# Attention beside a ternary feed-forward layer: gate and up kept as signs, the weights and half of the layer norm behind the first heads

## The chip, the cores and the metric

The kernel runs on one core of one Trainium2 chip. The metric is the device time of one execution in microseconds (us), and the median of several runs is compared. A core has a matrix engine (TensorE, PE), a vector engine (VectorE, DVE), a scalar engine for activations (ScalarE, ACT), a general engine (GpSimd, POOL), an engine that mostly issues DMAs (SyncE, SP), and 16 DMA engines. Each engine works off its own instructions in order, and instructions of different engines wait for each other by semaphores.

## The reference

The input x holds 2 sequences of 1024 tokens with 512 features, in f32. All of it, shortened:

```python
xn = layernorm(x)                       # over the 512 features, no affine part
q, k, v = split(xn @ w_qkv.T + b_qkv)   # 32 heads of 16 features
scores = q @ k.T / 4 + slope[head] * (key - 1023)   # ALiBi
scores = where(causal, scores, -1e9)
s = softmax(scores) @ v                 # per head
s = s @ w_out.T + b_out
# octonion layer: w has 8 components; M[k, i] is +w[j] or -w[j], with j given by k and i
ternary(w) = scale * clip(round(w / scale), -1, 1)   # scale = mean |w|
gate, up = xn @ M(ternary(w_gate)), xn @ M(ternary(w_up))   # 512 -> 8 x 170 = 1360
g = silu((silu(gate) * up) @ M(ternary(w_down)))            # 1360 -> 512
out = x + s * g
```

Ternary weights are kept as -1, 0 and 1, and the scale is multiplied in when a product is read out. The 512 by 1360 matrices of gate and up consist of 8 by 8 blocks, each a signed copy of one of the 8 components.

## The kernel before

The hidden width of 1360 makes 11 tiles `mt` of 128 (the last has 80 rows). The 2048 tokens make 16 tiles of 128 for the layer norm and 4 blocks `tb` of 512 for the feed-forward part. Everything is emitted in one long function. PE keeps the order in which its instructions are emitted. The order on the other engines, and the semaphores, are set by the scheduler of the framework, from priorities and data dependencies.

**Head.** `load_x` (L174) fetches the tokens and `normal` (L203) normalises them: statistics on DVE, Sqrt on ACT (L211), scaling on DVE (L214). `norm_item` (L354) transposes four blocks of 128 on PE (tile ptx) and copies them out with ACT (L360) into xnT. `load_wq` and `compact_wq` (L117 to L134) bring the q and k weights of two pairs of heads (wqr) and pack them on POOL into wq. `add_ring` (L139) makes the operand tiles, four q_stack and five k_stack, and fills their fixed rows with memsets (L142 to L147). q and k are kept as two parts, high and low, which add up to the f32 value.

**Attention.** Work goes in 32 units: sequence, group of four heads, half of the queries. `qk_items` (L417) computes q and k of two groups (pqk L436) and splits them (st: ACT L448, DVE L449). They go to DRAM and come back arranged as stacks by DMAs of the SP queue (`fill_q`, `fill_k`, L470 to L490). `max_items` (L492) makes the scores once (s L504) for their row maxima (DVE mp L514, scr L517). `place_max` (L543) transposes the maxima (pm) and ACT copies them to mr (L556), which four small POOL DMAs place into q_stack (L558). `exp_step` (L568) makes the scores again (s L578, mask L589) and ACT exponentiates them into p (L593). `value_step` (L595) multiplies with v (po L606), where v comes from `v_items` (L378, pv L391), and `normalise` (L619) divides. `out_items` (L645) is the output projection of one block.

**Ternary weights.** For each of w_g, w_u and w_d: `load_weight` (L259) loads 64 rows and once more with neighbouring components swapped; `ternary_sum` and `ternary_total` (L271, L277) compute the scale from wsum (DVE L274) through a product on PE (tot, L280); `ternary_signs` (L287, DVE L292 and L293) leaves -1, 0 or 1. `expand` (L295) makes 8 signed copies for each of four row blocks on ACT (L302), through two buffers "m". For gate and up, `expand_in` (L307) writes the full matrices from there into the DRAM array mw by POOL DMAs (L311, L315). For down, `turn_down` (L319) transposes first, four tiles at a time (ptd L329, ACT md, POOL L333).

**The planner.** At the time of writing the program, a loop with a rough model of engine times chooses what PE does next. Attention steps are taken in order. `side` is a list of other PE work with positions counted in steps from which it may be taken and by which it is due. `behind` is a queue of work that `later` appends, taken one at a time when what it needs is known (`next_behind`).

**Tail.** For each block of 512 tokens `split` (L1181) makes the high and low part of xnT (POOL L1189, DVE L1190). For the first block `load_fw` (L1193) fetches for each `mt` a tile fw with twelve slots of 128 columns: four gate, four up, four down. Eight of the eleven use the freed stack tiles. All four blocks use the same fw. `gate_up` (L1198) makes the products pg and pu (L1206), silu on ACT (L1215), the product on DVE (L1217) and the split hs on ACT and POOL (L1222, L1223). `down` (L1226, pd L1240) follows two `mt` behind. `load_rest` (L1260) fetches what the result needs.

Of the kernel before, what the change touches and what calls it, by code (L numbers as in the profile page):

```python
# [59 lines left out]
def kernel(  # L60
# [52 lines left out]
    mw = dram.tile([NM, P, 12, P], F32, name="mw")  # L113
# [25 lines left out]
    def add_ring(pool, qs, ks):  # L139
        for n in range(qs):  # L140
            q = pool.tile([P, 4, 512], F32R, name=f"q_stack{len(q_ring)}")
            nc.gpsimd.memset(q[64:128].bitcast(F32), 0.0)  # L142
            nc.gpsimd.memset(q[64:66].bitcast(F32), 1.0)
            q_ring.append(q)
        for n in range(ks):
            k = pool.tile([P, 4, 512], F32R, name=f"k_stack{len(k_ring)}")
            nc.gpsimd.memset(k[64:128].bitcast(F32), -1.0)  # L147
            k_ring.append(k)
# [20 lines left out]
    tmp = head.enter_context(tc.tile_pool(name="tmp", bufs=2))  # L169
# [4 lines left out]
    def load_x(t, eng):  # L174
        if t < 8:

            tag = ("ot", "ot", "oT", "oT", "y", "y", "posb", "scr")[t]
            xt = wk.tile([P, D], F32, tag=tag, name=f"xt_{t}", bufs=2 - t // 6)
        else:
            xt = tmp.tile([P, D], F32, tag="xt", name=f"xt_{t}", bufs=4)  # L180
        eng.dma_start(out=xt, in_=x[t * P : (t + 1) * P, :])
        x_tiles[t] = xt

    for t in range(8):
        load_x(t, nc.sync)
    load_wv(0)
    load_wq((0, 0), nc.scalar)
    al_sb = tmp.tile([P, HID], F32, tag="q", name="al", bufs=1)[0:H, 0:S]
    nc.gpsimd.dma_start(out=al_sb, in_=calibi)
    for n in range(2):  # L190
        for i in range(4):
            nc.gpsimd.dma_start(
# [4 lines left out]
            )  # L197
    nc.gpsimd.dma_start(out=mask, in_=cmask)
    nc.gpsimd.dma_start(out=bv_sb, in_=bv.partition_broadcast(P))

# [58 lines left out]
    def load_weight(src, name):  # L259
        if name == "g":  # L260
            w = vp.tile([P, 8, H8], F32, tag="v", name="w_g")
        else:
            w = tmp.tile([P, 8, H8], F32, tag="w", name=f"w_{name}")
        nc.sync.dma_start(out=w[0:64].rearrange("p j o -> p (j o)"), in_=src)
        pairs = src.rearrange("p (j s o) -> p j s o", s=2, o=H8)
        swapped = w[64:128].rearrange("p (j s) o -> p j s o", s=2)
        for n in range(2):
            nc.sync.dma_start(out=swapped[:, :, n, :], in_=pairs[:, :, 1 - n, :])
# [18 lines left out]
    def ternary_signs(name):  # L287
# [3 lines left out]
        q = tmp.tile([P, HID], F32, tag="q", name=f"q_{name}", bufs=1)  # L291
# [3 lines left out]
    def expand(name, kt, dtype):  # L295

        w = w_tiles[name]
        signs = sgn["d" if name == "d" else "i"]
        m = tmp.tile([P, 8, H8], dtype, tag="m", name=f"m_{name}_{kt}")

        for k in range(8):
            nc.scalar.activation(  # L302
                m[:, k, :], w[:, k ^ kt * 2, :], AF.Identity, scale=signs[:, kt, k : k + 1]
            )
        return m

    def expand_in(name, kt):  # L307
        m = expand(name, kt, F32R).rearrange("p k o -> p (k o)").bitcast(F32)
        slot = kt + (4 if name == "u" else 0)
        full = HID // P  # L310
        nc.gpsimd.dma_start(  # L311
            out=mw[0:full, :, slot, :].rearrange("m p n -> p m n"),
            in_=m[:, 0 : full * P].rearrange("p (m n) -> p m n", n=P),
        )
        nc.gpsimd.dma_start(out=mw[full, :, slot, 0 : HID - full * P], in_=m[:, full * P : HID])  # L315

    downs_box = {}

    def expand_down(kp):  # L319
        downs_box["nat"] = expand("d", kp, F32)  # L320

    def turn_down(kp, first):

        nat = downs_box["nat"].rearrange("p k o -> p (k o)")
        last = min(first + 4, NM)
        pt = ps_m.tile([P, 4, P], F32, tag="m", name=f"ptd_{kp}_{first}")
        for mt in range(first, last):
            fs = min(P, HID - mt * P)
            pe(nc.tensor.transpose(pt[:fs, mt - first, :], nat[:, mt * P : mt * P + fs], ident))  # L329
        md = tmp.tile([P, 4, P], F32R, tag="md", name=f"md_{kp}_{first}")  # L330
# [3 lines left out]
            out=mw[first : first + full, :, 8 + kp, :].rearrange("m p n -> p m n"),  # L334
            in_=md[:, 0:full, :].bitcast(F32),
        )
        if last == NM:
            fs = HID - (NM - 1) * P
            nc.scalar.copy(md[:fs, full, :], pt[:fs, full, :])
            nc.gpsimd.dma_start(out=mw[NM - 1, 0:fs, 8 + kp, :], in_=md[:fs, full, :].bitcast(F32))  # L340

    def alibi_parts():

        for n in range(2):
            part = tmp.tile([P, 8, H8], F32R, tag="m", name=f"al_{n}")
            part = part.rearrange("p k o -> p (k o)")[0:H, 0:S]
# [5 lines left out]
            nc.gpsimd.dma_start(out=al_dram[n], in_=part.bitcast(F32))  # L352
# [394 lines left out]
    for b in range(B):  # L747
        for hh in range(2):
            n = 2 * b + hh
            u = 8 * n  # L750
            if n == 0:
# [3 lines left out]
                max(u - 7, -1),  # L755
                u - 1,
                lambda n=n: n < 2 or unit_of(vals, V[0]) >= 8 * (n - 1),
            )
        for gp in range(2 - 2 * b, NP):
# [6 lines left out]
                lambda n=n: n < 2 or fills[0] >= 4 * (2 * n - 2),  # L766
            )
        for n, qc in enumerate((0, 1) if b + 1 < B else (1, 0)):
# [10 lines left out]
            )  # L779

# [19 lines left out]
    lead_in, behind = [], []  # L800
    grown, known = [0.0], {}
# [7 lines left out]
    def later(emit, model=None, need=None, cost=0, kind="none"):  # L809
        behind.append((emit, model, need, cost, kind))  # L810

    def grow(t):
        grown[0] = max(grown[0], t, now[0]) + 3500
        return grown[0]
# [4 lines left out]
    def weight(name, last):  # L819
# [11 lines left out]
        for kt in range(4):  # L831
            later(
                lambda kt=kt: expand_down(kt) if last else expand_in(name, kt),
                lambda kt=kt: set_known(("e", name, kt), grow(known["w", name])),
            )
            for f in range(0, NM if last else 0, 4):
                later(lambda kt=kt, f=f: turn_down(kt, f), None, ("e", name, kt), 436, "t")
# [9 lines left out]
    def end_head():  # L847
        head.close()
        add_ring(ctx.enter_context(tc.tile_pool(name="late", bufs=1)), 2, 3)

    qk, vs = qk_items(0, 0), v_items(0, 0)
    alibi_parts()
    for t in range(4):
        normal(t)
    compact_wq((0, 0))
    add_ring(early, 1, 1)
    for t in range(4, 8):
        normal(t)
    known.update({("n", t): 5500 + 1600 * t for t in range(8)})
    for name, w in (("g", wg), ("u", wu)):  # L860
        load_weight(w, name)
    add_ring(early, 1, 1)
    make_mask()
    make_signs()
    known.update({("l", "g"): 25000, ("l", "u"): 30000, ("l", "d"): 35000})
    for t in range(8, 12):
        later(lambda t=t: load_x(t, nc.sync))
    later(lambda: load_weight(wd, "d"))
    later(lambda: nc.sync.dma_start(out=bo_sb, in_=bo.partition_broadcast(P)))
    later(lambda: nc.sync.dma_start(out=wo_sb, in_=wo.rearrange("(k p) n -> p k n", p=P)))  # L870
# [8 lines left out]
    weight("g", False)  # L879
    weight("u", False)  # L880
    more_tokens(range(8, 12))
    later(lambda: [load_x(t, nc.sync) for t in range(12, 16)])
    weight("d", True)
    more_tokens(range(12, 16))
    later(end_head)
    side = [(d, ok or (lambda: True), it) for d, ok, it in lead_in + side]
# [47 lines left out]
    def try_fill():  # L934
# [4 lines left out]
        if n == 1 and len(q_ring) < 4 or part == 2 and len(k_ring) < 2:  # L939
# [153 lines left out]
    def next_behind():  # L1093
        while behind and not behind[0][3] and known.get(behind[0][2], 0) <= now[0]:
            emit, model = behind.pop(0)[:2]
            emit()
            if model:
                model()
        if not behind or not behind[0][3]:
            return []  # L1100
        emit, model, need, cost, what = behind[0]

        def go():
            behind.pop(0)
            emit()
            run_pe("F", ready, cost)
# [260 lines left out]
```

## Time and profile before

| | before |
|---|---|
| median of 3 runs | 1224.62 us |
| lowest, highest | 1218.01, 1227.27 us |
| profiled execution, its own time | 1222.66 us |
| its span | 1220.9 us |
| PE busy | 1094.6 us (90%) |
| DVE, ACT, POOL busy | 600.5, 508.3, 233.1 us |
| DMA | 113.36 MB, 93 GB/s on average |

The profile describes one execution. Busy time counts the instructions of an engine, and the idle time before an instruction is put down to what it waited for. L12 is line 12 of the kernel before. A DMA is listed by where its data go and come from (mw<-m_g). The page divides the span into 40 equal slices with a digit of tenths for each engine, and another for the granted PE clock.

### The profile page before, as it was taken

The page shows a single profiled execution, that of the slowest core. Times are in us where ns is not written, and L with a number is a line of the kernel's source. Part 1 is how long each engine was busy: PE and PEld are TensorE (multiplying, and loading weights), DVE is VectorE, ACT ScalarE, POOL GpSimd, SP SyncE. Part 2 cuts the span into 40 slices and gives each one's busy share as a digit, 9 for nine tenths or more (in the row PEclk, how much of TensorE's full clock was granted, in tenths as well). Part 3 has the DMA queues.
Part 4 walks back from the last instruction along what each step waited for, and adds up shares of the span by engine and source line. Part 5 has one row for each costly group of instructions (what it writes and reads, how often), then busy time and mean ns, then how long its engine had stood idle before and what let it go on. Part 6 is the DMA issues. An engine that isn't in the chain of part 4 may idle for free.

```text
span 1220.9 us, 16626 instructions
## 1 busy us (share of the span) xinstructions
PE 1094.6 (90%) x5714; PEld 686.8 (56%) x5714; DVE 600.5 (49%) x1640; ACT 508.3 (42%) x1131; POOL 233.1 (19%) x398
## 2 busy tenths in 40 slices
PE   4728879999799999998999999999989999999997
PEld 2414535555455555554655555555455777777775
DVE  6516506765565656666656654666732113131221
ACT  1263653345255544453543544446553222222222
POOL 6431450200111011020101000000110113232222
PEclk9868989999799999999999999999989999999998
DMA  9864456441731635416416332742217111112020
GB/s 260 220 174 138 143 91 113 110 79 40 144 59 24 114 58 127 98 52 133 74 55 128 60 74 57 173 81 41 62 49 242 42 53 51 53 35 69 20 85 35
DMA packets 78372, 113.36 MB, mean 93 GB/s; under 512 B 29472, under 2 KB 33056, under 8 KB 78288
## 3 DMA queue, kind: packets, MB, share of 16 engines
q1 hardware_dynamic: 68704, 94.10, 34.5%
q0 software_dynamic: 9296, 17.16, 4.9%
q8 instruction: 45, 0.74, 0.3%
q10 hardware_dynamic: 288, 1.05, 0.3%
q14 instruction: 39, 0.32, 0.1%
HBM read 73.76 MB, written 37.98 MB: 92 GB/s over the span
## 4 chain that ended last, share of the span: by engine, by line
PE 69%; DMA 10%; DVE 7%; issue 5%; POOL 4%; ACT 4%; SPq 0%; DVEq 0%; ACTq 0%; POOLq 0%
PE s L578 12%; PE s L504 12%; PE po L606 11%; PE pqk L436 6%; PE pg L1206 6%; PE pu L1206 5%; PE pd L1240 5%; DMA q_stack<-mr 5%; PE pout L675 4%; DVE scr L517 3%; PE pv L391 2%; PE s L589 2%; PE pm L549 1%; DVE mp L514 1%; DMA mw<-m_g 1%
## 5 line engine op out<-in xcount | busy, mean ns | idle before, releaser
L593 ACT ACTIVATE p<-s 128x512 f32<-128x512 f32 (+3 forms) x768 | 323.4, 495 | 313.9 <-PE s L589 217.1
L504 PE MATMUL s<-k_stack,q_stack 126*128 126x512 f32 (+3 forms) x768 | 306.6, 439 | 13.5 <-DVE mx L517 5.6
L578 PE MATMUL s<-q_stack,k_stack 128*128 128x512 f32 (+3 forms) x768 | 248.6, 388 | 25.4 <-DMA q_stack<-mr 19.0
L504 PEld LDWEIGHTS s<-k_stack,q_stack 126*128 126x128 f32 x768 | 141.2, 192 | 127.8 <-DVE mx L517 54.3
L514 DVE TENSOR_REDUCE mp<-s 128x1 f32<-128x512 f32 x256 | 169.0, 686 | 83.3 <-PE s L504 81.7
L578 PEld LDWEIGHTS s<-q_stack,k_stack 128*128 128x128 f32 x768 | 141.9, 193 | 96.9 <-ACT p L593 33.1
L517 DVE CUSTOM_DVE_ANT_0 scr<-s,mask 128x128 f32<-128x128 f32 (+3 forms) x256 | 125.1, 489 | 125.2 <-PE s L504 107.5
L517 DVE CUSTOM_DVE_ANT_0 scr<-s,mask,mp 128x128 f32<-128x128 f32 (+3 forms) x256 | 140.7, 550 | 85.2 <-PE s L504 67.2
L558 POOL DMA_DIRECT2D q_stack<-mr x128 | 63.6, 503 | 522.1 <-ACT mr L556 411.1
L606 PE MATMUL po<-p,v 128*32 128x512 f32 (+3 forms) x1536 | 148.2, 498 | 0.0
L436 PE MATMUL pqk<-xnT,wq 128*128 128x512 f32 x256 | 135.2, 632 | 12.7 <-ACT mr L556 6.0
L1217 DVE SCALAR_TENSOR_TENSOR h<-pu,sc_u,sg 128x512 f32<-128x512 f32 (+1 forms) x44 | 33.0, 751 | 168.8 <-PE pu L1206 163.0
L391 PE MATMUL pv<-wv,xnT 128*128 128x256 f32 x256 | 74.6, 399 | 25.0 <-ACT xnT L360 23.8
L1223 POOL TENSOR_TENSOR hs<-h,hs 128x512 fp32r<-128x512 f32 (+1 forms) x44 | 56.9, 1292 | 198.8 <-ACT hs L1222 198.8
L606 PEld LDWEIGHTS po<-p,v 128*32 128x32 f32 x1536 | 42.8, 110 | 65.8 <-issue 55.5
L1215 ACT ACTIVATE sg<-pg,sc_g 128x512 f32<-128x512 f32 (+1 forms) x44 | 30.3, 688 | 103.0 <-PE pg L1206 98.1
L436 PEld LDWEIGHTS pqk<-xnT,wq 128*128 128x128 f32 x256 | 46.1, 200 | 39.5 <-issue 22.3
L589 PE MATMUL s<-mask,ident 128*128 128x128 bf16 x512 | 66.7, 225 | 0.0
L391 PEld LDWEIGHTS pv<-wv,xnT 128*128 128x128 f32 x256 | 45.1, 194 | 34.5 <-ACT xnT L360 24.2
L675 PE MATMUL pout<-wo_sb,oT 128*128 128x512 f32 x128 | 61.9, 600 | 0.9 <-ACT oT L666 0.5
L1222 ACT CAST hs<-h 128x512 fp32r<-128x512 f32 (+1 forms) x44 | 27.2, 619 | 75.4 <-DVE h L1217 75.4
L449 DVE SCALAR_TENSOR_TENSOR st<-pqk,bqk_sb,st 128x512 fp32r<-128x512 f32 x32 | 23.8, 747 | 45.1 <-ACT st L448 44.9
(147 smaller groups left out, 1116.2 us busy)
## 6 DMA issues: line engine op xcount, KB each, us to landing
sp<-st SPq DMA_DIRECT2D x32, 512.0 KB, 3.9
q_stack<-sp SPq DMA_DIRECT2D x128, 128.0 KB, 6.1
k_stack<-sp SPq DMA_DIRECT2D x128, 128.0 KB, 4.9
wqr<-in_wqk_dram POOLq DMA_DIRECT2D x14, 512.0 KB, 6.0
xt<-in_x_dram SPq DMA_DIRECT2D x16, 256.0 KB, 8.4
att<-o SPq DMA_DIRECT2D x32, 128.0 KB, 4.8
ot<-att SPq DMA_DIRECT2D x16, 256.0 KB, 2.6
proj<-y SPq DMA_DIRECT2D x16, 256.0 KB, 3.3
```

The source lines that it names most:

```text
L391: nc.tensor.matmul(ps[:, 0:256], lhsT=xnT[:, c, b * S + kt * P : b * S + (kt + 1) * P], rhs=wv_tiles[2 * b + hh][:, c, :], start=(c == 0), ...
L436: nc.tensor.matmul(ps, lhsT=wq_tiles[b, gp][:, kt, which, :], rhs=xnT[:, kt, b * S + c * 512 : b * S + (c + 1) * 512], start=(kt == 0), st ...
L504: nc.tensor.matmul(ps[:, :n], lhsT=q_of(b, g, qc)[0 : NR - 2, i, tl * P : (tl + 1) * P], rhs=k_of(b, g, c)[0 : NR - 2, i, :n], start=True, ...
L514: nc.vector.tensor_reduce(pm, ps, AX.X, ALU.max)
L517: nc.vector.tensor_tensor_reduce(out=scr[:, :n], in0=ps[:, :n], in1=mask[:, 512 - n : 512], scale=1.0, scalar=pm if qc else -3.0e38, op0=A ...
L558: nc.gpsimd.dma_start(out=q[NR - 2 : NR, i, :].bitcast(F32), in_=mr[2 * i : 2 * i + 2, :].bitcast(F32),)
L578: nc.tensor.matmul(ps[:, :w], lhsT=k[0:NR, i, kt % 4 * P : (kt % 4 + 1) * P], rhs=q[0:NR, i, 512 - w : 512], start=True, stop=(kt < 4 * qc),)
L589: pe(nc.tensor.matmul(ps[:, 0:P], lhsT=ident16, rhs=mask16, start=False, stop=True))
L593: nc.scalar.activation(p_tiles[b, g, qc, kt][:, i, :w], ps[:, :w], AF.Exp, scale=0.25)
L606: nc.tensor.matmul(po[32 * i : 32 * i + 32, 512 - w : 512], lhsT=v[:, kt, h * VC : h * VC + 32], rhs=pr[:, i, :w], start=(kt == 0), stop=( ...
L675: nc.tensor.matmul(ps, lhsT=turned[t][:, c, :], rhs=wo_sb[:, c, :], start=(c == 0), stop=(c == KD - 1),)
L1206: nc.tensor.matmul(ps[:fs, :], lhsT=fw[mt][:, n0 + kt, 0:fs], rhs=part[:, kt, :], start=(kt == 0 and n == 0), stop=(kt == KD - 1 and n == 1),)
```

## The change

Gate and up are no longer expanded in the head. Their signs (64 by 1360 for each) are stored in `signs_dram` by `keep_signs`, and mw shrinks from 12 slots to the 4 of down. When the exps reach the fifth unit from the end, `fetch_signs` reads the signs back, again once straight and once swapped, into a free wqr and a free v slot. `expand_in(mt)` then writes the signed pieces for one hidden tile into fw directly, gate on ACT and up on DVE, in program order two tiles ahead of the first block's products. `load_fw` fetches only down's four slots. The tiles for fw are ordered anew, and the split of the second and fourth block moves into the wqr and v slots and from `mt` 4 to `mt` 9.

In the head, weights are loaded one after the other through one v slot and by POOL's queue instead of SP's. The bias lines go by SP instead of POOL. Entries of `behind` now have a position before which they are not taken: up's weight 0.6 of an average unit, down's 1.2, the four turns of down from 1.4 on in steps of 0.3, tokens 8 to 15 from 3 units on. Entries that cost PE nothing now come ahead of other choices. Most ring tiles are made early, two memsets on DVE. The last k_stack waits for the end of down's weight, and v of later heads for that tile. One Sqrt is issued ahead of the first loads. The buffers of the pool "tmp" go from two to one, and md uses the "ot" slots.

```diff
-    mw = dram.tile([NM, P, 12, P], F32, name="mw")
+    signs_dram = dram.tile([2, 64, HID], F32, name="signs_dram")
+    mw = dram.tile([NM, P, 4, P], F32, name="mw")
...
-            nc.gpsimd.memset(k[64:128].bitcast(F32), -1.0)
+            eng = nc.vector if len(k_ring) < 2 else nc.gpsimd
+            eng.memset(k[64:128].bitcast(F32), -1.0)
...
-    tmp = head.enter_context(tc.tile_pool(name="tmp", bufs=2))
+    tmp = head.enter_context(tc.tile_pool(name="tmp", bufs=1))
...
+        tag = ("ot", "ot", "oT", "oT", "y", "y", "posb", "scr")[t if t < 8 else 2 + t % 4]
+        xt = wk.tile([P, D], F32, tag=tag, name=f"xt_{t}", bufs=1 if t in (6, 7) else 2)
...
+    warm = wk.tile([P, 1], F32, tag="sd", name="warm")
+    nc.scalar.activation(warm, eps, AF.Sqrt)
     for t in range(8):
         load_x(t, nc.sync)
+    load_wq((0, 0), nc.scalar)
     load_wv(0)
-    load_wq((0, 0), nc.scalar)
-    al_sb = tmp.tile([P, HID], F32, tag="q", name="al", bufs=1)[0:H, 0:S]
-    nc.gpsimd.dma_start(out=al_sb, in_=calibi)
     for n in range(2):
         for i in range(4):
-            nc.gpsimd.dma_start(
+            nc.sync.dma_start(
...
+    add_ring(early, 1, 2)
...
-        if name == "g":
-            w = vp.tile([P, 8, H8], F32, tag="v", name="w_g")
-        else:
-            w = tmp.tile([P, 8, H8], F32, tag="w", name=f"w_{name}")
-        nc.sync.dma_start(out=w[0:64].rearrange("p j o -> p (j o)"), in_=src)
+        w = vp.tile([P, 8, H8], F32, tag="v", name=f"w_{name}")
+        nc.gpsimd.dma_start(out=w[0:64].rearrange("p j o -> p (j o)"), in_=src)
         pairs = src.rearrange("p (j s o) -> p j s o", s=2, o=H8)
         swapped = w[64:128].rearrange("p (j s) o -> p j s o", s=2)
         for n in range(2):
-            nc.sync.dma_start(out=swapped[:, :, n, :], in_=pairs[:, :, 1 - n, :])
+            nc.gpsimd.dma_start(out=swapped[:, :, n, :], in_=pairs[:, :, 1 - n, :])
...
-    def expand(name, kt, dtype):
-
-        w = w_tiles[name]
-        signs = sgn["d" if name == "d" else "i"]
-        m = tmp.tile([P, 8, H8], dtype, tag="m", name=f"m_{name}_{kt}")
-
-        for k in range(8):
+    def keep_signs(n, name):
+        nc.sync.dma_start(
+            out=signs_dram[n], in_=w_tiles[name][0:64].rearrange("p j o -> p (j o)")
+        )
+
+    nat = {}
+
+    def expand_down(kp, half):
+
+        if half == 0:
+            nat[kp] = tmp.tile([P, 8, H8], F32, tag="m", name=f"m_d_{kp}")
+        for k in range(4 * half, 4 * half + 4):
             nc.scalar.activation(
-                m[:, k, :], w[:, k ^ kt * 2, :], AF.Identity, scale=signs[:, kt, k : k + 1]
-            )
-        return m
-
-    def expand_in(name, kt):
-        m = expand(name, kt, F32R).rearrange("p k o -> p (k o)").bitcast(F32)
-        slot = kt + (4 if name == "u" else 0)
-        full = HID // P
-        nc.gpsimd.dma_start(
-            out=mw[0:full, :, slot, :].rearrange("m p n -> p m n"),
-            in_=m[:, 0 : full * P].rearrange("p (m n) -> p m n", n=P),
-        )
-        nc.gpsimd.dma_start(out=mw[full, :, slot, 0 : HID - full * P], in_=m[:, full * P : HID])
-
-    downs_box = {}
-
-    def expand_down(kp):
-        downs_box["nat"] = expand("d", kp, F32)
+                nat[kp][:, k, :],
+                w_tiles["d"][:, k ^ kp * 2, :],
+                AF.Identity,
+                scale=sgn["d"][:, kp, k : k + 1],
+            )
 
...
-        md = tmp.tile([P, 4, P], F32R, tag="md", name=f"md_{kp}_{first}")
+            pe(nc.tensor.transpose(pt[:fs, mt - first, :], m[:, mt * P : mt * P + fs], ident))
+        md = wk.tile([P, 4, P], F32R, tag="ot", name=f"md_{kp}_{first}")
...
-                max(u - 7, -1),
+                u - 4,
                 u - 1,
-                lambda n=n: n < 2 or unit_of(vals, V[0]) >= 8 * (n - 1),
+                lambda n=n: len(k_ring) == 5
+                and unit_of(vals, V[0]) >= 8 * (n - 1)
+                and (n < 2 or not behind),
...
-                lambda n=n: n < 2 or fills[0] >= 4 * (2 * n - 2),
+                lambda b=b, n=n: n < 2 or fills[0] >= 4 * (2 * n - 2) and (b == 0 or not behind),
...
-        behind.append((emit, model, need, cost, kind))
-
-    def grow(t):
-        grown[0] = max(grown[0], t, now[0]) + 3500
-        return grown[0]
+        behind.append((emit, model, need, cost, kind, int(begin[0] * (size[0] + size[1]) / 2)))
...
-        add_ring(ctx.enter_context(tc.tile_pool(name="late", bufs=1)), 2, 3)
+        add_ring(ctx.enter_context(tc.tile_pool(name="late", bufs=1)), 0, 1)
...
-    alibi_parts()
-    for t in range(4):
+    for t in range(8):
         normal(t)
-    compact_wq((0, 0))
-    add_ring(early, 1, 1)
-    for t in range(4, 8):
-        normal(t)
-    known.update({("n", t): 5500 + 1600 * t for t in range(8)})
-    for name, w in (("g", wg), ("u", wu)):
-        load_weight(w, name)
-    add_ring(early, 1, 1)
+        if t == 3:
+            compact_wq((0, 0))
+            alibi_parts()
+    known.update({("n", t): 7500 + 1600 * t for t in range(8)})
+    known.update({("l", "g"): 40000, ("l", "u"): 44000, ("l", "d"): 50000, "x": 48000})
+    add_ring(early, 1, 0)
     make_mask()
     make_signs()
-    known.update({("l", "g"): 25000, ("l", "u"): 30000, ("l", "d"): 35000})
+    load_weight(wg, "g")
+    add_ring(early, 2, 2)
     for t in range(8, 12):
-        later(lambda t=t: load_x(t, nc.sync))
-    later(lambda: load_weight(wd, "d"))
-    later(lambda: nc.sync.dma_start(out=bo_sb, in_=bo.partition_broadcast(P)))
-    later(lambda: nc.sync.dma_start(out=wo_sb, in_=wo.rearrange("(k p) n -> p k n", p=P)))
+        load_x(t, nc.sync)
+    later(lambda: nc.gpsimd.dma_start(out=bo_sb, in_=bo.partition_broadcast(P)), None, "x")
+    later(lambda: nc.gpsimd.dma_start(out=wo_sb, in_=wo.rearrange("(k p) n -> p k n", p=P)))
...
-    weight("g", False)
-    weight("u", False)
-    more_tokens(range(8, 12))
-    later(lambda: [load_x(t, nc.sync) for t in range(12, 16)])
-    weight("d", True)
-    more_tokens(range(12, 16))
+    weight("g")
+    later(lambda: keep_signs(0, "g"))
+    later(lambda: load_weight(wu, "u"))
+    begin[0] = 0.6
+    weight("u")
+    later(lambda: keep_signs(1, "u"))
+    later(lambda: load_weight(wd, "d"))
+    begin[0] = 1.2
+    weight("d")
+    for kp in range(4):
+        begin[0] = 1.4 + 0.3 * kp
+        spread(kp, 0)
+        spread(kp, 1)
+        for f in range(0, NM, 4):
+            later(lambda kp=kp, f=f: turn_down(kp, f), None, ("e", kp), 436, "t")
     later(end_head)
+    for t in range(8, 16):
+        begin[0] = 3 + (t - 8) * 0.6
+        more_tokens([t])
+        if t < 12:
+            later(lambda t=t: load_x(t + 4, nc.sync))
...
+    def next_behind(pos):
+        if not behind or behind[0][5] > pos:
+            return []
+        emit, model, need, cost, what, _ = behind[0]
...
+        return [(ready, 0.5 if not cost else 4.5, 0, go)] if ready < HELD else []
...
+    w_again = []
+
+    def fetch_signs():
+
+        w_again.append(wqp.tile([P, 8, H8], F32, tag="wqr", name="w_again_0"))
+        w_again.append(vp.tile([P, 8, H8], F32, tag="v", name="w_again_1"))
+        for n, w in enumerate(w_again):
+            pairs = signs_dram[n].rearrange("p (j s o) -> p j s o", s=2, o=H8)
+            swapped = w[64:128].rearrange("p (j s) o -> p j s o", s=2)
+            nc.sync.dma_start(out=w[0:64].rearrange("p j o -> p (j o)"), in_=signs_dram[n])
+            for m in range(2):
+                nc.sync.dma_start(out=swapped[:, :, m, :], in_=pairs[:, :, 1 - m, :])
...
+        if not w_again and unit_of(exps, E[0]) >= NU - 5:
+            fetch_signs()
...
-            xh, xl = (
-                pp.tile([P, KD, 512], F32R, tag="p", name=f"{n}_{tb}") for n in ("xh", "xl")
-            )
+            if "odd" not in halves:
+                halves["odd"] = (
+                    wqp.tile([P, KD, 512], F32R, tag="wqr", name="xh_odd"),
+                    vp.tile([P, KD, 512], F32R, tag="v", name="xl_odd"),
+                )
+            xh, xl = halves["odd"]
...
-        nc.sync.dma_start(out=fw[mt][:, 0:8, 0:fs].bitcast(F32), in_=mw[mt, :, 0:8, 0:fs])
-        nc.sync.dma_start(out=fw[mt][:fs, 8:12, :].bitcast(F32), in_=mw[mt, 0:fs, 8:12, :])
+        nc.sync.dma_start(out=fw[mt][:fs, 8:12, :].bitcast(F32), in_=mw[mt, 0:fs])
+
+    def expand_in(mt):
+
+        fs = min(P, HID - mt * P)
+        for n in range(2):
+            for kt in range(KD):
+                f = 0
+                while f < fs:
+                    k, o = divmod(mt * P + f, H8)
+                    size = min(fs - f, H8 - o)
+                    dst = fw[mt][:, 4 * n + kt, f : f + size]
+                    src = w_again[n][:, k ^ kt * 2, o : o + size]
+                    sign = sgn["i"][:, kt, k : k + 1]
+                    if n:
+                        nc.vector.tensor_scalar_mul(dst, src, sign)
+                    else:
+                        nc.scalar.activation(dst, src, AF.Identity, scale=sign)
+                    f += size
 
...
+    for mt in range(2):
+        expand_in(mt)
...
+        if n + 2 < NM:
+            expand_in(n + 2)
+        if mt == NM - 2 and tb + 1 < NT // 512:
             split(tb + 1)
```

## The prediction

> **What bounds the kernel now.** I read the page's slices first. They show TensorE (PE) full from about 200 us on, and a head in which it is not.
>
> ```profile
> span 1220.9 us, 16626 instructions
> PE 1094.6 (90%) x5714; PEld 686.8 (56%) x5714; DVE 600.5 (49%) x1640; ACT 508.3 (42%) x1131; POOL 233.1 (19%) x398
> ...
> PE   4728879999799999998999999999989999999997
> ...
> PEclk9868989999799999999999999999989999999998
> ```
>
> Each digit stands for 30.5 us. The third PE digit, a 2, covers 61 to 92 us. Then I asked for busy time by stretch (columns: length, PE, weight load, DVE, ACT, POOL, granted PE clock, DMA share, GB/s):
>
> ```profile
> 0.00:66.00 66.00, 39.29 (x126) 24.14 (x126) 39.73 (x85) 16.94 (x41) 34.22 (x114) 0.92 0.94 234
> 66.00:89.00 23.00, 0.07 (x1) 0.07 (x1) 0.00 (x0) 13.99 (x42) 8.37 (x10) 0.58 0.58 179
> 0.00:200.00 200.00, 132.30 (x562) 79.41 (x562) 91.96 (x238) 83.33 (x209) 77.95 (x172) 0.86 0.70 171
> 200.00:960.00 760.00, 714.04 (x4116) 415.19 (x4115) 451.05 (x1335) 360.12 (x822) 83.19 (x171) 0.98 0.41 87
> 960.00:1221.00 261.00, 248.28 (x1039) 192.15 (x1037) 57.50 (x67) 64.82 (x100) 71.96 (x55) 0.98 0.15 51
> ```
>
> PE idles 200 − 132.3 = 67.7 us before 200, 46.0 us (6%) in the middle, 12.7 us in the tail: over half of all idle time is in the first sixth. One wait makes a third of it, as the waits of 60 to 90 us show (waiter <- releaser: total, times, longest):
>
> ```profile
> PE pv L391 <- ACT xnT L360: 23.8, 1, 23.8
> POOL mw L311 <- ACT m_g L302: 16.9, 4, 8.4
> ACT m_g L302 <- DMA mw<-m_g: 7.1, 1, 7.1
> ACT m_u L302 <- DMA mw<-m_g: 2.5, 1, 2.5
> ACT m_u L302 <- DMA mw<-m_u: 2.4, 1, 2.4
> ```
>
> The transposed tokens' copy, 0.48 us long, stands on ACT behind the gate's and up's expansions, and those wait for their two buffers to be written to DRAM. The chain of waits there (start, length, what):
>
> ```profile
> 61.56 8.38 DMA mw<-m_g
> ...
> 74.02 3.66 DMA mw<-m_g
> ...
> 77.92 2.73 ACT m_u L302 x8
> 80.65 0.29 issue
> 80.94 0.43 POOL mw L311
> 81.37 0.53 issue
> 81.90 3.67 DMA mw<-m_u
> ...
> 88.41 0.48 ACT xnT L360
> ```
>
> The middle of the kernel is PE's, so the change is worth what it leaves of those 67.7 us, less what it adds later.
>
> **What the Trainium skill says.** "TensorE: Matmul & The Clock Gate", Part 1: The HAM clock gate: an idle PE falls to half clock and takes some microseconds of work to win it back. The trace agrees: granted clock 0.58 in the stall, 0.66 in 80 to 100. "ScalarE: Activation LUTs", What ACT_TABLE_LOAD costs: exp and sqrt lie in different sets, and each change pays a load near 1.28 us and a drain as long. The trace shows 1283 ns loads, three of them, with no drain beside. "DMA: Bandwidth & Descriptors", on the SWDGE path: a DMA from GpSimd has about 2 us of fixed cost, mostly the receipt of the write. The trace's 4 KB q_stack<-mr takes 2.6 us.
>
> **The change part by part.** The profiled execution took 1222.66 us around its 1220.9 us span; the sum is made against it. The median, 1224.62, is 0.2% above.
>
> (1) *Start.* Before, the first pqk products wait for the compact weights (L130, 8 copies, 2.40 us) on POOL, and these stood behind the issue of the bias lines, which waits 7.3 us for DVE. Now the bias loads go by SP. The first products start at about 17.9 us (before 21.1). The second batch of transposes came at 36.5 us, held (PE 12.1 + 6.2 us of waiting for DVE) behind the statistics of tokens 8 to 11, whose loads came late in a DMA load of 0.93. In the emitted order these statistics still stand early, but no weight loads and sums are among them, and their loads are ordered sooner. It comes at about 27.4, the second pqk half ends at 42.9 (before 50.9), the first maxima start at 51 (before 58.7). Of the 26.7 us that PE idled up to 66, I leave 14, in this rounded way: 26.7 less 7.7 of earlier start less about 5 us of waits in between.
>
> (2) *The stall.* Gone: gate's and up's 64 expansion instructions (10.7 and 10.8 us of ACT by their rows) and their 16 writes leave the head. What is late next is the max work: DVE's 0.68 us reduction per tile against PE's 0.44 us product, up to the first q_stack<-mr. I leave 3.5 us of idle for that and 2 for the landing of those four small DMAs (2.0 us of issue, 2.6 landing), plus 2.5 for the first exps.
>
> (3) *Up's weights.* load_weight goes from SP to POOL, one weight at a time in one v slot. In the emitted order w_u's load stands behind the compact copy of the third pair of heads, which waits for PE's last product of the pair (call it T), 8 copies (2.4 us) and two wqr loads (0.53 us each); issued near T + 4, landing after 6.5 (wqr's 6.0, w_d's 8.6). On DVE the wait for it (wsum_u) stands in the middle of the maxima of the last key tiles, so mp, scr, mx and the PE products behind their PSUM buffers wait. PE has work to about T + 7.1 and DVE goes on at T + 10.5 + 1.6 for the sum: PE loses about 6 us (3 to 8).
>
> (4) *Down's weights.* The same: w_d's load waits for the store of up's signs on SP, itself behind a k_stack fill that needs PE's product at T2, and stands on POOL behind four q_stack<-mr issues. It lands near T2 + 13.5; wsum_d then 1.56 us, and tot_d on PE is in order. PE loses 8 us (5 to 11).
>
> (5) *Down's turning*, 32 expansions on ACT (11.3 us, as before) in four bursts, each in two halves, among the exps. md now has two "ot" buffers, and its third copy waits for a DMA (2.8 us landing): 4 × 1.2 = 5 us on PE. Before, the same work cost waits of 6.0 and 3.5 us, which lie in the 67.7.
>
> (6) *Tokens 8 to 15* are transposed later, one by one. The Sqrt of the last four falls among the Exps: by the order ACT changes there and back three times, 6 loads × 1.28 = 7.7 us on ACT. ACT is 47% busy there, but the exps follow each other on PE's path: half, 4 us, is charged; 0 to 8.
>
> (7) *Ring memsets.* The late 3.5 + 3.5 + 5.3 us on the chain become one, which has 12 us of lead over its need. Nothing is left of it; without the lead it would cost 5.3.
>
> (8) *Tail.* The gate's 77 pieces go on ACT and the up's on DVE, in full 0.33 us for 170 columns (8 in 2.73 us), so about 0.25 for half as many. Emitted two hidden tiles ahead, they are hoisted: some 44 gate pieces, 11 us, lie on ACT within the last three units, where ACT has 49.6 of 91 us busy and each delays an exp behind it. DVE's 24 (5 us by 0.2) lie where DVE has 49.7 of 91. I charge 3 + 1.5 = 4.5 us; bounds 0 (all beside products, 5.55 us of PE per hidden tile of a block) and 10. DRAM reads of the first block fall from 768 to 256 KB per tile: gain at most 2, taken as nothing. fetch_signs' six issues on SP cost 3.3 us of a queue, nothing on PE; split at mt 9 still has 11 us ahead of its need.
>
> *Sum.* Idle in what was the first 200 us: 14 + 3.5 + 2 + 2.5 + 6 + 8 + 5, and 6% of the 92 us that are then steady, 5.5: 46.5 against 67.7, a gain of 21.2. The slow clock took, by slices of 20 us, busy × (1 − clock), about 17 us from 20 to 200; half of this was around the stall: gain 8. Less 4 (Sqrt) and 4.5 (tail): 20.7. 1222.66 − 20.7 = 1202.
>
> **The rivals.**
> A, the forecast: 1202 us, its own range 1190 to 1213.
> B, the weights' waits are covered: PE has more products in hand at T and T2 than I count (the order lets value and score products be taken first), so (3), (4) and (5) give back 19 and the clock 3: 1180. For it: six PSUM buffers of score tiles and the value work; against: DVE's order is fixed, and every max behind it waits.
> C, the gain is eaten by the many small waits: (3) and (4) at their upper ends (+5), the bursts of (5) doubled (+5), Sqrt and tail at theirs (+9.5): 1222.
> D, slower: loads of up and down on POOL's queue land 24 us after they may be issued, since three DMAs queue behind 1 MB of wqr reads and share the engines with fills (131 GB/s moved in 89 to 200: 1.7 MB at half of that takes 26 us). Each wait then grows by 17.5 us, and the clock falls again, 2 us each: 1202 + 39 = 1241. It decides from about 24 us of landing each. For it: w_g's halves took 10.3 us in the crowded head. Against: 6.0 for wqr later.
>
> **How the numbers follow.** A measurement of this kernel can tell about 1% from no change: 1212.4 to 1236.9 around the median. Chances: A 0.48, B 0.20, C 0.18, D 0.14. A and B fall beyond 1% but for 0.04 of A; C is within, but for 0.04 of either side in all. Faster 0.66, same 0.18, slower 0.16. Range: B's 1180 less 10 for PE slack that I can't see, to 1232, which takes C whole and leaves most of D out.
>
> **What would show it.** Right: no PE wait over 8 us between 50 and 90; first exp at 60 to 75 us (before 124.5); waits of DVE for w_u and w_d of 5 to 12 us, PE idle of 6 and 8 beside them; nine table loads; PE idle of 45 to 50 us in what was the first 200; a middle still at 6%; ACT expansions in the last units at 0.25 to 0.33 us. Wrong: DVE waiting over 20 us for a weight (D), no wait for them at all (B), or PE idle over 10% in the last three units, where (8) would be the term that I mis-sized.

## The result, and the profile after

The changed kernel takes 1228.05 us, the median of 20 runs, beside 1225.65 us of 20 runs of the kernel before: 1.0018 of it, with a 95% interval of 0.9998 to 1.0038. That is no change that can be told. The forecast was 1202 us. The profiled execution of the changed kernel took 1222.24 us, that of the kernel before 1222.66, so the two traces can be laid side by side; both lie below the median of their kernel.

The slices of the page show what went and what came:

```profile
span 1220.4 us, 16672 instructions
PE 1096.8 (90%) x5714; PEld 690.5 (57%) x5714; DVE 626.0 (51%) x1714; ACT 512.9 (42%) x1146; POOL 222.3 (18%) x381
...
PE   4876868998999799998999999999989999999997
...
PEclk9888979998799999999999999999999999999999
```

The 2 in the third place of PE's row is gone. In its neighbourhood stand several 6s and 8s: the idle time is not gone but spread. Busy time by stretch (columns: length, PE, weight load, DVE, ACT, POOL, granted PE clock, DMA share, GB/s):

```profile
0.00:66.00 66.00, 42.57 (x146) 27.29 (x146) 48.80 (x97) 11.80 (x26) 37.91 (x109) 0.95 0.76 209
108.00:120.00 12.00, 3.51 (x10) 1.75 (x9) 3.44 (x5) 0.69 (x1) 1.34 (x3) 0.81 0.90 247
147.00:163.00 16.00, 2.30 (x12) 1.76 (x10) 3.55 (x7) 1.67 (x4) 3.79 (x7) 0.69 0.72 144
0.00:200.00 200.00, 137.93 (x607) 80.20 (x607) 113.35 (x262) 64.94 (x153) 69.49 (x167) 0.90 0.58 149
```

PE idles 62.1 us before 200 us, against 67.7 before and 46.5 forecast. Of this, 8.5 us lie between 108 and 120, and 13.7 between 147 and 163. The waits of DVE and of PE in 100 to 170 us name the cause:

```profile
DVE wsum_d L273 <- DMA w_d<-in_wd_dram: 11.5, 1, 11.5
DVE wsum_u L273 <- DMA w_u<-in_wu_dram: 7.7, 1, 7.7
...
PE tot_d L279 <- DVE wsum_d L273: 13.7, 1, 13.7
PE s L495 <- DVE mp L505: 8.5, 1, 8.5
```

DVE stands at the sum of up's weight until the load lands. PE then wants a score buffer that DVE's maximum (mp), queued behind the sum, has to free. For down PE itself needs the sum. The chain of waits shows why up's load is late (start, length, what):

```profile
104.25 1.95 POOL wq L131 x8
106.20 0.29 issue
106.48 0.47 POOL wqr L121
106.95 0.07 issue
107.02 0.53 POOL wqr L121
107.55 9.68 DMA w_u<-in_wu_dram
```

The load is issued behind the packing of q and k weights and two loads on POOL's queue, and takes 9.68 us to land. For down's load the tile's own lines tell more (first and last start in us):

```profile
L267 POOL DMA_DIRECT2D w_d<-in_wd_dram x2: 631/641/651, 150.0 to 154.2; - x2
L263 POOL DMA_DIRECT2D w_d<-in_wd_dram x1: 549/549/549, 149.5 to 149.5; - x1
L273 DVE TENSOR_REDUCE wsum_d<-w_d x1: 1562/1562/1562, 159.9 to 159.9; 64x1 f32<-64x1360 f32 x1
L291 DVE TENSOR_SCALAR q_d<-w_d,sc_d x1: 929/929/929, 162.6 to 162.6; 128x1360 f32<-128x1360 f32 x1
...
DMA to landing us min/median/max: 6.7/10.4/10.4
```

The sum reads the first 64 rows, which the first DMA (L263) brings alone. It was issued at 149.5 us and landed 10.4 us later, and the sum started at once. The last DMA was held on POOL for 3.6 us by an older load of wqr, but it landed at 160.9 us, before q_d needed it at 162.6, so that hold cost nothing.

To see what a wait costs, I took PE's products from the traces, weighed each with the median duration of its kind, and noted how much sooner than the kernel before each kernel reaches the same sum. This lead at five times, in us (E1, E2 and E12 are experiments below):

| at | changed | E1, neither load | E2, early loads | E12, no load of up |
|---|---|---|---|---|
| 100 | 30.9 | 30.9 | 37.5 | 31.1 |
| 130 | 16.1 | 32.6 | 32.7 | 33.0 |
| 160 | 9.1 | 26.3 | 26.3 | 12.6 |
| 340 | 5.1 | 25.4 | 25.3 | 13.4 |
| 1180 | 0.6 | 20.6 | 18.1 | 5.1 |

At 100 us the change has won 31 us. The first wait takes 15, by 340 us another 11 are gone, and at the end nearly all. Without either load the lead shrinks too, from 32.6 to 25.4 us by 340 and to 20.6 at the end. (A lead counts whatever product is done, in any order, so single values swing by some us; the 37.5 of E2 is the least certain.)

### The profile page after: what moved, and what is told of

It is laid out like the page before. It is cut to its first block, busy times and chain, and to the rows that moved or that the text cites. A ratio compares the mean times of both kernels' runs of the same rounds, so it can differ in the third digit from the quotient of the medians.

```text
span 1220.4 us, 16672 instructions
## 1 busy us (share of the span) xinstructions
PE 1096.8 (90%) x5714; PEld 690.5 (57%) x5714; DVE 626.0 (51%) x1714; ACT 512.9 (42%) x1146; POOL 222.3 (18%) x381
## 4 chain that ended last, share of the span: by engine, by line
PE 67%; issue 11%; DMA 8%; DVE 7%; ACT 3%; POOL 3%; SPq 0%; DVEq 0%; POOLq 0%; ACTq 0%
PE s L569 12%; PE s L495 11%; PE po L597 10%; PE pqk L427 6%; PE pg L1239 6%; PE pu L1239 5%; PE pd L1273 5%; PE pout L666 4%; PE pv L382 3%; DVE scr L508 2%; DMA q_stack<-mr 2%; PE s L580 2%; DVE xt L216 1%; ACT p L584 1%; PE pm L540 1%
## 5 line engine op out<-in xcount | busy, mean ns | idle before, releaser
L569 PE MATMUL s<-q_stack,k_stack 128*128 128x512 f32 (+3 forms) x768 | 253.3, 395 | 19.7 <-DMA q_stack<-mr 14.2
L495 PEld LDWEIGHTS s<-k_stack,q_stack 126*128 126x128 f32 x768 | 143.7, 196 | 139.5 <-DVE mx L508 59.0
L427 PEld LDWEIGHTS pqk<-xnT,wq 128*128 128x128 f32 x256 | 45.4, 198 | 31.1 <-issue 18.7
L382 PEld LDWEIGHTS pv<-wv,xnT 128*128 128x128 f32 x256 | 45.4, 193 | 12.6 <-issue 5.1
L439 ACT ACTIVATE st<-pqk,bqk_sb 128x512 fp32r<-128x512 f32 x32 | 21.9, 689 | 68.1 <-PE pqk L427 59.6
```

What stands on the lines that cost most here:

```text
L382: nc.tensor.matmul(ps[:, 0:256], lhsT=xnT[:, c, b * S + kt * P : b * S + (kt + 1) * P], rhs=wv_tiles[2 * b + hh][:, c, :], start=(c == 0), ...
L427: nc.tensor.matmul(ps, lhsT=wq_tiles[b, gp][:, kt, which, :], rhs=xnT[:, kt, b * S + c * 512 : b * S + (c + 1) * 512], start=(kt == 0), st ...
L495: nc.tensor.matmul(ps[:, :n], lhsT=q_of(b, g, qc)[0 : NR - 2, i, tl * P : (tl + 1) * P], rhs=k_of(b, g, c)[0 : NR - 2, i, :n], start=True, ...
L569: nc.tensor.matmul(ps[:, :w], lhsT=k[0:NR, i, kt % 4 * P : (kt % 4 + 1) * P], rhs=q[0:NR, i, 512 - w : 512], start=True, stop=(kt < 4 * qc),)
```

## Experiments

My theory, W: the head's gain is spent in the two waits for loads. The rival, L: the lead is lost up to 300 us anyway, to work that was put off.

**E1, neither load.**

```diff
-    later(lambda: load_weight(wu, "u"))
+    later(lambda: w_tiles.update(u=w_tiles["g"]))
...
-    later(lambda: load_weight(wd, "d"))
+    later(lambda: w_tiles.update(d=w_tiles["g"]))
```

> The changed kernel without the loads of w_u and w_d: up and down take gate's tile in their place, so the work on it stays, and both waits for a load are gone (the order of PE is the same). Theory W (the head's gain is spent in the two waits for these loads on DVE, whose trace shows lead over the kernel before falling from 29 to 16 us at the first and from 23 to 3 us at the second): some 25 to 30 us less than the changed kernel, near 1200 us. Rival L (the lead is lost in 170 to 300 us anyway, to transposes, table loads and work that was put off; without the waits it is lost there): not below 1218 us.

Measured: 1201.83 us, 0.9766 of before (0.9706 to 0.9826). This is the number of W and not that of L. PE's idle time over the whole trace falls from 123.6 us (span less busy time) to 101.6, by as much as the waits of 8.5 and 13.7 us. A part of L is left: the lead in the table still shrinks by 12 us after 130 us without the loads.

**E12, without the load of up alone** (the first of the two lines above).

> The changed kernel without the load of w_u alone (up takes gate's tile); w_d's load, its queue and its wait stay as they are. By the traces the wait for w_u costs 12 us (8.5 of PE's idle time, 3.4 by the half clock after it) and that for w_d 18 (13.7 and 4.3). If these two are separate terms: 12 us less than the changed kernel, 1216, with an 11 to 12 us wait of DVE for w_d left in the trace. If taking one away makes the other longer: 1221 or more. If the first carries most: 1208.

Measured: 1216.51 us, 0.9891 (0.9865 to 0.9918), as the sum of separate terms had it. The other wait is still there:

```profile
DVE wsum_d L273 <- DMA w_d<-in_wd_dram: 11.7, 1, 11.7
...
PE tot_d L279 <- DVE wsum_d L273: 13.9, 1, 13.9
```

So by the medians up's wait costs 1228.05 − 1216.51 = 11.5 us, and down's 1216.51 − 1201.83 = 14.7 us. By the ratios, each taken to the runs of the kernel before beside it, it is 15 to 16 us for each; the intervals leave some 4 us either way for the first and 8 for the second.

**E2, early loads**, with the whole computation.

```diff
+        if name == "u":
+            w = wo_sb.rearrange("p k n -> p (k n)")[:, 0:HID].rearrange("p (j o) -> p j o", o=H8)
+        else:
+            w = vp.tile([P, 8, H8], F32, tag="v", name=f"w_{name}")
...
     load_weight(wg, "g")
+    load_weight(wu, "u")
...
     later(lambda: keep_signs(0, "g"))
-    later(lambda: load_weight(wu, "u"))
+    later(lambda: load_weight(wd, "d"))
...
-    later(lambda: load_weight(wd, "d"))
+    later(lambda: nc.gpsimd.dma_start(out=wo_sb, in_=wo.rearrange("(k p) n -> p k n", p=P)))
...
-    part = wk.tile([64, 1], F32, tag="wsum", name=f"wsum_{name}")
+    part = wk.tile([64, 1], F32, tag="wsum", name=f"wsum_{name}", bufs=1)
```

> The full computation: w_u is loaded in the head into the tile that later holds the output projection's weights, w_d right after gate's signs are stored, and one buffer for the sums keeps w_d's sum on DVE from being taken before up's total. PE's order is the same. Theory W: both waits gone, within 5 us of the kernel without the loads, near 1202 us. Rival L: as for the kernel without the loads, 1218 us or more. If the 0.7 MB of w_u delay the head instead, first exps come 4 us later.

Measured: 1204.66 us, 0.9792 (0.9742 to 0.9842), and once more, beside E6 and E7:

> The kernel with the early loads once more, as the base of the two beside it: 0.979 of the kernel before, as measured (1204.7 us).

1205.76 us, 0.9817 (0.9791 to 0.9843). PE does the same instructions in the same order as in the changed kernel, so some 2% hang on when two loads of 0.7 MB each are issued and on where their sums stand on DVE: the one buffer also puts down's sum behind up's total. These parts weren't run apart. No wait for a weight is left. PE's waits of 100 to 170 us begin:

```profile
PE pm L543 <- DVE st L443: 3.5, 1, 3.5
PE s L498 <- DVE mx L511: 2.8, 4, 1.5
```

**E3, loads on the SP queue; E4, later places.** In E3 the three `dma_start` of `load_weight` go from `nc.gpsimd` to `nc.sync`. E4:

```diff
-    begin[0] = 0.6
+    begin[0] = 1.1
...
-    begin[0] = 1.2
+    begin[0] = 2.0
...
-        begin[0] = 1.4 + 0.3 * kp
+        begin[0] = 2.2 + 0.3 * kp
```

> Only the queue of the three weight loads goes back from POOL to SP; PE's order is the same. Theory W, if the queue is what makes them late: w_u is issued some 7 us earlier, since it no longer stands behind the packing of weights, and w_d some 3; DVE's waits fall from 7.7 and 11.5 us to about 1 and 6, and the time falls by 10 to 15 us, to about 1214. If the slot's release is what counts, waits and time stay within 3 us of the changed kernel (1228).

> Only positions change: up's weight from 0.6 to 1.1 units, down's from 1.2 to 2.0, down's turns from 1.4 to 2.2 on. On DVE up's sum stays at its row, down's moves 21 rows later. Theory W: the first wait stays (7.7 us of DVE), the second goes, the time falls by about 14 us to 1214. Rival L: what is put off is paid later, within 3 us of 1228.

E3 measured 1214.73 us, 0.9882 (0.9831 to 0.9934); in its trace, that of the slowest of four runs, DVE's waits were 2.0 us for up and 8.3 for down. The time is the expected one, but up's wait didn't shrink in the expected way. Its load was issued at 106.5 us, 1.0 us sooner and not 7, since on SP it stands behind a store of q and k (sp<-st). It landed 2.4 us sooner, and the scheduler had put the sum behind three more maxima, so that DVE came to it at 112.8 us instead of 109.5. That the queue made up's load late is thus not shown. Down's load waits for the storing of up's signs in any case; it was issued 4.7 us after that store instead of 6.5.

E4 measured 1221.62 us, 0.9936 (0.9908 to 0.9963): 6.2 us of wait left for up, 1.3 for down. This is neither the 1214 of W nor the 1225 or more of L. In its trace PE's idle time fell from 123.6 to 109.5 us, about as much as down's wait was long, but PE was busy for 1109.5 us instead of 1096.8 with the same number of products. Some 7.5 us of this are half clock, by the estimate used under the next heading; the rest stays open. A position in the planner moved PE's total of up (from 138.8 to 142.6 us), but not the sum on DVE (117.2 us in both): that stayed where the scheduler had it, ahead of its data.

**E6, no table swaps.** On top of E2:

```diff
-        nc.scalar.activation(sd, mv[:, 1:2], AF.Sqrt, bias=eps)
+        nc.scalar.activation(sd, mv[:, 1:2], AF.Sqrt if t < 12 else AF.Identity, bias=eps)
```

> Early loads, and for tokens 12 to 15 ACT takes Identity instead of Sqrt, which leaves out the root there: same instructions on every engine but for six table loads. If the swaps cost PE what the forecast charged: 4 us less than the base, about 1200.5. If other work hides them: within 1.5 us of it. Full price of six loads: 7.7 us.

Measured: 1201.17 us, 0.9773 (0.9751 to 0.9795), 4.6 us below E2 beside it. The charge of 4 us was near, though the intervals just touch.

**E7, expansions doubled.** On top of E2 a loop `for _ in range(2):` around the write of each piece in `expand_in`.

> Early loads, and each piece of gate and up is written twice in the tail (another 24 us of ACT, 15 of DVE). If the forecast's 4.5 us for the expansions is right and grows in proportion: 4 to 6 us more than the base, about 1209. The traces so far lose 1 to 3 us of lead from 820 us on: then 1 to 3 us more. If the second copies push ACT past its free time: 10 us or more.

Measured: 1206.86 us, 0.9807 (0.9780 to 0.9835), against 0.9817: not to be told from nothing, nor, with intervals this wide, from the 4 to 6 us. It fits expansions that lie mostly beside other work, and doesn't prove it.

**E8, the kernel before without the expansions.** In `weight` of the kernel before, `expand_in` is not called, and `load_fw` fills the eight slots of gate and up from down's.

> The kernel before without the expansion of gate and up and its writes (their slots of fw are filled from down's part instead): how much the head's expansions cost where they stood. If the stall of 23.8 us and its slow clock were all theirs: 25 to 32 us less than before, about 1198, near the kernel with early loads (1204.7). If something else held the head as long, such as the loads and the turning of down: 1210 or more.

Measured: 1202.48 us, 0.9784 (0.9760 to 0.9809). The expansions in the head cost the kernel before 26 us, about what the wait of 23.8 us and the half clock after it suggest. (The planner's order on PE differs in 229 of 5714 places.) The sign path is worth this, and then loses it.

**E9, root on DVE; E11, the same with the loads on SP.** E9 is E2 with the reciprocal root of tokens 12 to 15 by three Newton steps of

```python
nc.vector.scalar_tensor_tensor(sd, rs, va, rs, ALU.mult, ALU.mult)
nc.vector.tensor_scalar(sd, sd, -0.5, 1.5, ALU.mult, ALU.add)
nc.vector.tensor_tensor(rs, rs, sd, ALU.mult)
```

> Early loads, and the reciprocal root of tokens 12 to 15 by three Newton steps on DVE (11 small operations of 0.15 us each, variance near 1 in these inputs), full computation: no Sqrt among the exps. If the six table loads are what the kernel without the swaps saved (4.6 us): 1201 us, 0.978 of before; the 6.6 us of DVE work hidden. If that DVE work is on the path: no better than early loads alone (1205).

> Early loads by the SP queue instead of POOL, and the root on DVE. If w_u's and w_d's three issues on POOL still cost something: 1 to 3 us less than the root on DVE alone, near 1199. If not: the same, 1201.

E9: 1202.47 us, 0.9806 (0.9765 to 0.9847), not to be told from E2. E11: 1197.56 us, 0.9755 (0.9717 to 0.9793), the fastest version here, 2.5% below both kernels; its parts are too small to be told apart by these runs.

**E10, fills on ACT.** On top of E2, q_stack tiles 2 and 3 get their fixed rows by

```python
nc.scalar.activation(q[p0:p1].rearrange("p a n -> p (a n)"),
                     ident[p0:p1, 0:1].to_broadcast([p1 - p0, 2048]),
                     AF.Identity, scale=0.0, bias=value)
```

> Early loads, and the fixed rows of two q_stack tiles are written by ACT instead of POOL. One DVE scaling of a token tile took 10.1 us at 20.9 us in the changed kernel (0.53 us elsewhere), while POOL did memsets from 22.0 to 32.8 us. Theory: DVE is held by POOL's memsets; then that operation falls to 4 us or less, the second batch of transposes comes some 3 us sooner, and the time falls by 2 to 4 us. Rival: DVE is slowed by the DMAs (share 0.8 to 0.9) and stays slow: within 1.5 us of early loads. ACT's fills may delay the first Sqrts by 2 us each and eat the gain.

Measured: 1209.16 us, 0.9844 (0.9805 to 0.9883): no gain, and the theory's 4 us or less for DVE failed. The longest scaling took 6.38 us; in the two traces of the early loads, which are its base, it takes 6.94 and 5.50. On ACT the four fills of 1.9 us each and the Sqrts came ahead of the first copies of xnT, and the last of these Sqrts waited 5.6 us for DVE, until the long scaling had ended. So the first pqk product came at 30.8 us instead of 19, and PE waited 12.6 us for a copy of xnT. What it shows is under the last heading.

## Why the prediction was wrong

The mechanism was found: the stall goes, and two waits for loads come. What failed is the size of three terms, all taken too much in the kernel's favour: the start (1), the loads (3) and (4), and the clock, which was credited with a gain and brought none. The profiled execution took 1222.2 us, 20 above the forecast.

- *Step (1), the start: failed.* PE's idle time up to 66 us was 66 − 42.57 = 23.4 us where I left 14: 9.4 us. The first products came at 19.0 us (17.9 forecast), but the second transposes at 35.2, not 27.4. PE waited for the scaling of a token tile on DVE, as it had before (first line the changed kernel, second the one before):

```profile
PE ptx L350 <- DVE xt L216: 14.1, 3, 12.3
PE ptx L359 <- DVE xt L214: 12.6, 2, 12.1
```

I had put that wait down to late loads of tokens 8 to 11 and did not look at the one scaling that took long: 4.44 us before, 10.13 in the changed kernel. The last heading tells what it stood behind. What the start would be without it, no run shows.

- *Step (2), the stall: right.* It went, with the size that E8 measures. The first exp came at 84.4 us, not at 60 to 75: PE had taken value products first and then waited 6.5 us for a q_stack fill.
- *Steps (3) and (4), the loads: the place right, the size wrong.* I charged 6 + 8 us of idle PE; the trace has 8.5 + 13.7, beyond both upper ends (8 and 11). The loads took 9.7 to 10.4 us to land, where I took 6.5 from quieter rows although w_g's halves showed 10.3. (In E4, where it was issued 5 us later, the first DMA of w_d took 4.2 us.) E1 prices both waits at 26 us in all by the medians, where I charged 14.
- *The clock: failed.* I credited 8 us for the half clock around the stall, from the mean clock of slices of 20 us. Taken by the stretches in which half clock was granted, the one at the stall was long but nearly empty of work (first line; the kernel before), and two came behind the new waits (the changed kernel):

```profile
69.61:93.50 23.89, 4.57 (x14) 3.91 (x15) 0.76 (x3) 17.04 (x50) 11.09 (x13) 0.50 0.52 153
...
115.55:122.38 6.83, 2.92 (x5) 1.70 (x6) 4.01 (x5) 0.00 (x0) 0.00 (x0) 0.50 0.57 191
153.10:170.16 17.06, 7.28 (x27) 4.73 (x31) 7.64 (x17) 4.79 (x12) 0.69 (x2) 0.50 0.35 61
```

As an estimate, half of PE's busy time in such stretches is lost; what is left of its busy time over the whole trace is then nearly the same in both kernels (1069 and 1068 us). From 20 to 200 us PE was busy in them for 29.6 us before and 20.0 after, so the loss fell from 14.8 to 10.0: a gain of 4.8 us, not 8. From 200 to 960 us it rose from 8.7 to 17.4, which the sum has no term for; that is one execution of each, and its cause stays open. In all, PE's busy time rose by 2.2 us (1094.6 to 1096.8). "TensorE: Matmul & The Clock Gate" of the Trainium skill, Part 1, which I had cited for the old stall, applies to the new ones alike: half clock was granted late in both waits and behind them. But E1, without these waits, loses 11.4 us in the first 200 us by the same estimate, so a price of the new stalls in clock is not shown.

- *Step (5), down's turning: too dear by the trace.* One wait of 3.1 us for a copy of md where I charged 5. *Step (6), Sqrt: right* (4 charged; E6 4.6). *Step (7), ring memsets: nothing left, as forecast.*
- *Step (8), the tail: probably too dear.* I charged 4.5 us. ACT's busy time in 835 to 926 us rose from 49.60 to 60.84 us as foreseen, but PE's idle time there rose only from 6.5 to 8.5 us. Doubling the work (E7) added 1.1 us, which excludes neither nothing nor 4.5.

The two traces account for the miss of 20 us. PE's idle time before 200 us was 62.1 us and not 46.5: 15.6 more, of which the start has 9.4 and the loads 8.2 (22.2 − 14), and the rest is 2.0 less. PE's busy time rose by 2.2 us where 8 less were credited for the clock: 10.2 more. Its idle time after 200 us rose by 2.9 us where (6) and (8) charged 8.5: 5.6 less. 15.6 + 10.2 − 5.6 = 20.2.

In outcome this is rival C, but that C's 1222 came out is luck: it put 14.5 of its 19.5 us into (5), Sqrt and the tail, which cost no more than charged or little more. (3) and (4), which C gave 5 us more, took 8.2 more. In mechanism this part is D at a smaller size: loads on POOL's queue that land late. The start, the largest miss of idle time, is in none of the rivals. B was the kernel with both waits gone, which E2 shows to be worth 1205, not 1180. The range of 1170 to 1232 held the result; the chance of 0.18 for no change did not do it justice.

## What to carry to other kernels

A sum or a check of a load that is set by a scheduler ahead of the engine's main work is a wait of the main work: give the load a slot that is free early (here the tile of a weight not needed until much later), or tie the consumer to an instruction behind which its data are sure to be there. Price a load's landing by the row with the traffic that it will meet, and ask which of its DMAs the consumer reads: here the sum needed the first alone. When idle time is taken away, take the slow clock from PE's busy time only, and look at the slow clock of the whole kernel, not of the place alone.

## What the runs showed of the hardware

A DVE scaling of one token tile, 0.52 to 0.55 us in most places, took 10.13 us in the changed kernel while POOL filled ring tiles. DVE's and then POOL's timeline there (start, length, what):

```profile
20.93 10.13 DVE L216 TENSOR_SCALAR xt<-xt,mv,rs 128x512 f32<-128x512 f32 x1
...
22.00 3.57 POOL L143 MEMSET q_stack<- 64x2048 f32 x2
25.49 3.54 POOL L144 MEMSET q_stack<- 2x2048 f32 x2
28.98 3.82 POOL L149 MEMSET k_stack<- 64x2048 f32 x2
```

It ended at 31.06 us, 0.28 us after the first of the two k_stack memsets (30.78). The kernel before, whose page the forecast was made from, shows the same: the scaling ends at 31.36 us, 0.29 us after a memset (31.07).

```profile
26.92 4.44 DVE L214 TENSOR_SCALAR xt<-xt,mv,rs 128x512 f32<-128x512 f32 x1
...
29.27 1.80 POOL L147 MEMSET k_stack<- 64x2048 f32 x1
```

In E10, with fewer memsets on POOL, the two long ones do the same, the first of them 4 us sooner than in the changed kernel: the memsets end at 26.69 and 30.00, the scalings at 26.98 and 30.28.

```profile
20.60 6.38 DVE L226 TENSOR_SCALAR xt<-xt,mv,rs 128x512 f32<-128x512 f32 x1
...
27.93 2.35 DVE L226 TENSOR_SCALAR xt<-xt,mv,rs 128x512 f32<-128x512 f32 x1
...
23.13 3.57 POOL L159 MEMSET k_stack<- 64x2048 f32 x2
...
27.98 2.02 POOL L390 MEMSET v<- 128x2304 f32 x1
```

"SBUF — State Buffer" of the Trainium skill, section Who interferes with whom, says that a DVE `tensor_scalar` can need the pair of ports that it shares with GpSimd, and that whichever comes second is blocked for the other's whole instruction. Six ends of DVE operations 0.28 to 0.29 us behind the end of a POOL memset (these four, and 33.08 after 32.79 in E9, 33.06 after 32.78 in E2) agree that DVE stood still until a memset was done, and they speak against slow DMAs as the cause. Two things don't follow from the page: in the changed kernel the DVE operation had begun 1.1 us ahead of the first memset and yet was the one held, and it was passed over by several memsets in a row, to the end of the fifth. What held it at its start, when POOL was issuing DMAs, stays open, as does what the head would gain without the overlap: E10 lost time elsewhere.
